# The scales of a sequence, turned one resume later behind the last of their powers, in a convolution, attention and state-space kernel

## The chip, the cores and the metric

One core of one Trainium2 chip runs the whole kernel. The metric is the device time of one execution in microseconds (us), the median over several runs. The time before is the median of three.

## The reference

The input `x` is 4 images of 128 channels and 64 x 64 pixels, in float32. Layer 0 normalizes it by groups and adds three convolutions (7x7, 5x5, 3x3), a non-local attention block and the input. Layer 1 takes the 4096 pixels of an image as a sequence of tokens of 128 features, and the change lies there:

```python
t = _to_tokens(x)                       # 4 sequences, 4096 tokens, 128 features
t = t + _L1_attn_ref(_ln_t(t), ...)     # h_f + h_b, a scan forwards and one backwards
t = t + _L1_ffn_ref(_ln_t(t), ...)      # projection, batch norm, a sigmoid recurrence

def _ln_t(v, eps=1e-5):
    m = jnp.mean(v, axis=-1, keepdims=True)
    s = jnp.var(v, axis=-1, keepdims=True)
    return (v - m) / jnp.sqrt(s + eps)
```

Both halves of layer 1 begin with a layer norm over the 128 features of a token, so each token needs one scale, 1/sqrt(variance + eps). (The mean is taken care of in the weights, which the kernel centres.) `_L1_attn_ref` is a state-space layer in each direction: a projection, a convolution of 4 taps, gates, and a scan with per-token decays `dt` and `dA`. The time steps `dt` come from the normalized tokens through a softplus, that is from exponentials and logarithms.

## The kernel before, in words

**Layout.** `t` lies in the on-chip memory with the 128 features on the partitions and all 4 x 4096 tokens along the free axis. The scan of layer 1 is `mamba`: 4 sequences b of 32 steps i of 128 tokens each, 128 steps n in all. Four steps make a group G, and j = i % 4 is the place in the group. A step does `states`, `turn`, `scan`, `prepare` and `take` (L1011 to L1066) for its own tokens, and, depending on j, a part of the projections of the next group (`project_bwd`, `project_bc`, `project_fwd`, `project_z`, L891 to L951) or of the finishing of the last one (`squares`, `means`, `gate`, `back`, L1068 to L1150). The step of j=1 is the one with `px` (L928, read by VectorE in L938), `pm` (L1087, read by VectorE in L1089) and `pb` (L901).

**Scales.** `row_scales` is a generator. It first runs `row_statistics`: for each of eight blocks of 512 tokens TensorE transposes four tiles of 128 x 128 into PSUM (`ls_in`, L83), VectorE takes mean and variance (L85 to L89), and GpSimd raises variance + eps to the power of -0.5 (`mr`, L74); after each block it yields. When all blocks are done it turns the 128 x 32 scales into 32 x 128 with one TensorE transpose (`rs_t`, L101), ScalarE copies them out of PSUM (L103), and SyncE sends them to device memory (L104), from where they are read back as rows that are broadcast over the partitions (`spread`, L109).

It is called in four places:

- L481, for the first sequence, whose tokens layer 0 leaves early, resumed in the loops of the attention block.
- L1161, in `open_sequence`, which prepares sequence b+1 while sequence b is being scanned. The generator of the opening is resumed at the end of each step from i=4, twice per step in i=4 to 7, so that the eight blocks are done in i=4 to 7, and `rs_t` follows in i=8. Behind it come the broadcasts `tl<-scale` (L109), three empty resumes (L1163), the products of scale and token (`scaled`, L727, two per resume, on GpSimd), and then `steps` (L798 to L888): `pd` in i=16 (projection to dt, L811), `pdt` in i=17 (its transposes, L821, read by VectorE in L825), the absolute value and the exponential in i=18 (L832 to L837), the logarithm and what follows it up to `dA` in i=19 (L839 to L847), `pcs` and `pt` in i=20 (running sums, L860 to L867), `pr` and the store of them in i=21 (L879 to L885).
- L1172, in `ended`, for the sequence before the present one, whose tokens are final by then: resumed once a step from i=20, so its eight blocks are in i=20 to 27 and its `rs_t` in i=28.
- L1331, in `recurrence`, run through at once.

The last sequence has its own blocks of statistics ahead of the recurrence (L1268 to L1271): steps 24, 25, 28 and 29 of the last sequence do one block each, behind the resume of `ended`.

**What sets the order.** TensorE and ScalarE run the scan in the order in which the code issues their instructions (`manual_schedule`, L787 and L788), so a yield decides in which step, and behind what, an instruction stands. VectorE, GpSimd and SyncE are put in order by a scheduler. All three queues run strictly in order, each instruction waiting for what it needs. Products of the openings, the gates and the state updates `S` (L1026) share GpSimd. The opening, the statistics, the projections and `pm` take their PSUM buffers from one pool, `ring`, of three:

```python
ring = ctx.enter_context(tc.tile_pool(name="m_ring", bufs=3, space=PSUM))
...
pt = ring.tile([P, MT, GT, QT], F32, tag="big", name="pdt")
```

Of the kernel before, what the change touches and what calls it, by code (L numbers as in the profile page):

```python
# [70 lines left out]
def rsqrt(nc, k, out, in_):  # L71

    p, n = in_.shape
    nc.gpsimd.tensor_tensor(out, in_, k.neghalf[:p].to_broadcast([p, n]), ALU.pow)  # L74


def row_statistics(nc, k, ps, tag, pool, src, mr, parts=None):

    for j in range(mr.shape[1] // GT) if parts is None else parts:
        pt = ps.tile([P, GT, P], F32, tag=tag, name="ls_in")  # L80
        st = pool.tile([P, GT, nc.vector.BN_STATS_DIM], F32, tag="ls_st", name="ls_st")
        for i in range(GT):
            nc.tensor.transpose(pt[:, i, :], src[:, ds(j * NC + i * P, P)], k.ident)  # L83
        for i in range(GT):
            nc.vector.bn_stats(st[:, i, :], pt[:, i, :])  # L85
        for i in range(GT):
            nc.vector.bn_aggr(mr[:, j * GT + i, :], st[:, i, :])
        v = mr[:, bass.ts(j, GT), 1]
        nc.vector.tensor_scalar(v, v, LN_EPS, None, ALU.add)  # L89
        rsqrt(nc, k, v, v)  # L90
        yield


def row_scales(nc, k, ps, tag, pool, src, mr, mem, parts=None):

    yield from row_statistics(nc, k, ps, tag, pool, src, mr, parts)
    n = mr.shape[1]
    pt = ps.tile([n, P], F32, tag=tag, name="rs_t")  # L100
    nc.tensor.transpose(pt, mr[:, :, 1], k.ident)  # L101
    row = pool.tile([n, P], F32, tag="rs_row", name="rs_row", bufs=1)
    nc.scalar.copy(row, pt)  # L103
    nc.sync.dma_start(mem, row)  # L104
# [48 lines left out]
def conv_attention(nc, tc, k, a, t, B, H, W, flags, load, mem, loads):  # L153
# [22 lines left out]
    with ExitStack() as ctx:  # L176
# [272 lines left out]
        for n in range(N):  # L449
# [17 lines left out]
            for i, _ in enumerate(convolve(n // 2, q % 2)):  # L467
                if i == 0:
                    if q % 2 == 0 and n:
                        for m in (n - 2, n - 1):  # L470
                            finish(m, atts.pop(m))
                        cv.pop(n // 2 - 1)
                    atts[n] = divide(n, acc, es)
                if more:
                    part = keys(b + 1, i)
                    next(part)
                if i == 2 and n + 1 < N:
                    th = queries(n + 1)
                if i == 3 and n == NQ + 1:
                    mr = wk.tile([P, NT, 2], F32, tag="mr", name="mr", bufs=1)  # L480
                    stats = row_scales(nc, k, ps_c, "c", wk, t[:, 0:T], mr, mem)  # L481
                if i == 3 and n > NQ:
                    next(stats, None)
                if more:
                    run(part)
# [204 lines left out]
def mamba(nc, tc, k, a, t, B, T, vec, first=None, after=None, mr=None):  # L690
# [16 lines left out]
    with ExitStack() as ctx:  # L707
# [447 lines left out]
        def open_sequence(b):  # L1155

            src = t[:, b * T : (b + 1) * T]
            if b not in tls:
                mr = pre.tile([P, NT, 2], F32, tag="mr", name="mr", bufs=1)
                mem = dram.tile([NT, P], F32, tag="scale", name="scale")  # L1160
                yield from row_scales(nc, k, ring, "big", wk, src, mr, mem)  # L1161
                scales(b, mem)
                for _ in range(3):  # L1163
                    yield
            if b not in ready:
                yield from scaled(b)
                yield
            yield from steps(b, ready[b])

        def ended(b):  # L1170
            mr = pre.tile([P, NT, 2], F32, tag="mr2", name="mr2", bufs=1)
            return row_scales(nc, k, ring, "big", wk, t[:, b * T : (b + 1) * T], mr, after[b])  # L1172
# [375 lines left out]
```

## Time and profile before

| | before |
|---|---|
| median of three runs | 3434.59 us (3430.04 to 3438.03) |
| profiled execution, span | 3440.8 us, mean granted TensorE clock 0.980 |
| instructions | 43618 |

The median is what counts; the profiled execution took a little longer than it. The profile lists for each engine how long it was busy, and which groups of instructions took that time. The trace behind it gives the start and length of each instruction and, where its engine stood idle ahead of it, the length of that wait in brackets and what ended it (an engine, a tile, a line of the kernel). Layer 0 takes the first part of the span and the scan roughly from 1.9 to 3.3 ms; the share of ScalarE, VectorE and GpSimd differs much between the two, so averages over the span say little on the scan. All that the change moves in the scan lies in a few steps of each sequence, of some 10 us each, and is read from the timelines of those steps:

| `rs_t` of | start, us | wait of TensorE ahead of it, us |
|---|---|---|
| first sequence, in layer 0 | 1079.69 | 0 |
| next sequence, first opening, i=8 | 2024.34 | 0 |
| next sequence, second opening, i=8 | 2364.80 | 0 |
| `ended` for the third sequence, i=28 | 3261.86 | 5.38 |
| recurrence | 3309.94 | 0.79 |

### The profile page before, as it was taken

To read this page: it belongs to the slowest core of one execution; us is meant where nothing else is said; L and a number is where in the kernel's file an instruction comes from. 1 tells how busy PE (TensorE), PEld (TensorE's weight loads), DVE (VectorE), ACT (ScalarE), POOL (GpSimd) and SP (SyncE) were. 2 spreads that over 40 slices of the span, in tenths; PEclk is the share of its full clock that TensorE was granted. 3 is DMA by queue.
4 is the path that set the end of the run, shared out by engine and by line. 5 is a ranking of instruction groups with operands and counts; after the bars stand their busy time and mean duration, and the time that the engine had idled before them with its cause. 6 is when DMAs were issued, how large, how long until landed. Compare 5 with 4: busy or idle time off the path is not lost. (4 is left out here: it accounts for less than half of the span.)

```text
span 3440.8 us, 43618 instructions
## 1 busy us (share of the span) xinstructions
PE 3261.0 (95%) x16823; PEld 1717.0 (50%) x16823; DVE 2138.7 (62%) x3204; ACT 1557.9 (45%) x2060; POOL 1593.3 (46%) x1414
## 2 busy tenths in 40 slices
PE   7999999999999999999998899999999999999976
PEld 2554545555555555455554344444444444544445
DVE  7555445555545555455544676777677777777767
ACT  3323233323333333333322566666656566666556
POOL 3434332534343424242533265557446654565653
PEclk9999999999999999999999899999999999999988
DMA  4000000000000000000001233333333423333332
GB/s 164 1 1 1 1 1 1 0 1 1 1 1 1 0 1 1 1 1 1 1 1 48 74 111 80 96 87 111 86 81 96 111 80 81 95 94 89 85 109 99
DMA packets 91685, 162.71 MB, mean 47 GB/s; under 512 B 23822, under 2 KB 27534, under 8 KB 90316
## 3 DMA queue, kind: packets, MB, share of 16 engines
q1 hardware_dynamic: 90252, 158.53, 16.2%
q8 instruction: 134, 2.20, 0.3%
q10 hardware_dynamic: 1216, 1.31, 0.1%
q14 instruction: 83, 0.68, 0.1%
HBM read 149.97 MB, written 9.82 MB: 46 GB/s over the span
## 5 line engine op out<-in xcount | busy, mean ns | idle before, releaser
L369 ACT ACTIVATE ex<-pf 128x1024 f32<-128x1024 f32 x512 | 497.0, 1021 | 571.6 <-PE pf L367 559.3
L384 DVE TENSOR_TENSOR es<-es,ex 128x1024 f32<-128x1024 f32 x448 | 590.6, 1318 | 207.5 <-ACT ex L369 179.4
L367 PE MATMUL pf<-theta,phi 64*128 64x512 f32 x2048 | 513.3, 619 | 10.8 <-ACT ex L369 10.4
L319 PE MATMUL pm<-yf,w 128*128 128x256 f32 x2048 | 503.1, 380 | 0.0
L378 PE MATMUL acc<-ex,gT 128*64 128x512 f32 x2048 | 491.4, 606 | 0.2 <-ACT ex L369 0.2
L331 POOL TENSOR_TENSOR eo<-s 128x256 f32<-128x256 f32 x128 | 90.1, 725 | 782.4 <-ACT s L328 782.4
L319 PEld LDWEIGHTS pm<-yf,w 128*128 128x128 f32 x2048 | 383.9, 189 | 113.5 <-issue 54.3
L367 PEld LDWEIGHTS pf<-theta,phi 64*128 64x128 f32 x2048 | 174.0, 186 | 326.7 <-ACT ex L369 208.6
L1007 POOL TENSOR_TENSOR ct<-ct,Cst 128x512 f32<-128x512 f32 x128 | 181.3, 1417 | 323.0 <-DMA ct<-csmem 261.9
L334 DVE TENSOR_TENSOR eo<-eo,pm 128x512 f32<-128x512 f32 x64 | 44.0, 688 | 425.8 <-PE pm L319 397.1
L378 PEld LDWEIGHTS acc<-ex,gT 128*64 128x64 f32 x2048 | 127.5, 136 | 337.5 <-issue 327.2
L969 DVE TENSOR_TENSOR lt<-cs,lt 128x1024 f32<-128x1024 f32 x128 | 180.5, 1411 | 182.3 <-DMA lt<-csmem 171.7
L328 ACT COPY s<-pm 128x512 f32<-128x512 f32 x64 | 37.5, 585 | 498.6 <-PE pm L319 498.6
L286 POOL TENSOR_TENSOR yf<-yr 128x340 f32<-128x340 f32 x256 | 241.4, 963 | 4.9
L914 PE MATMUL px<-tl,wx_fwd 128*128 128x512 f32 x512 | 238.6, 609 | 0.0
L901 PE MATMUL pb<-tl,wbc_bwd 128*64 128x512 f32 x512 | 235.1, 601 | 0.0
L901 PE MATMUL pb<-tl,wbc_fwd 128*64 128x512 f32 x512 | 234.5, 601 | 0.0
L286 POOL TENSOR_TENSOR yr<-xp 128x700 f32<-128x700 f32 x64 | 100.4, 1569 | 277.8 <-PE pm L319 232.0
L1072 POOL TENSOR_TENSOR yT<-yT,zT 128x512 f32<-128x512 f32 x127 | 183.8, 1456 | 74.1 <-DVE yT L1059 58.7
L1006 DVE TENSOR_TENSOR lt<-lt,gm 128x1024 f32<-128x1024 f32 x128 | 187.6, 1465 | 1.3
L390 DVE RECIPROCAL att<-den 128x512 f32<-128x512 f32 x32 | 107.4, 3357 | 108.0 <-PE den L388 108.0
L319 PE MATMUL pm<-yr,w 128*128 128x256 f32 x512 | 162.6, 398 | 0.0
(263 smaller groups left out, 5488.1 us busy)
## 6 DMA issues: line engine op xcount, KB each, us to landing
lt<-csmem SPq DMA_DIRECT2D x128, 512.0 KB, 5.5
ct<-csmem SPq DMA_DIRECT2D x256, 128.0 KB, 5.3
rs<-m SPq DMA_DIRECT2D x31, 512.0 KB, 3.7
t<-in_x SPq DMA_DIRECT2D x4, 2048.0 KB, 28.5
rows<-after SPq DMA_DIRECT2D x32, 256.0 KB, 4.8
out<-t SPq DMA_DIRECT2D x4, 2048.0 KB, 11.4
tl<-scale SPq DMA_DIRECT2D x24, 256.0 KB, 6.4
w<-in_w7t SPq DMA_DIRECT2D x1, 3136.0 KB
```

Source lines behind the costliest of these rows:

```text
L286: nc.gpsimd.tensor_tensor(out, at(x), at(y), op)
L319: nc.tensor.matmul(pm[:, e, :], wt, src, start=(i == 0), stop=(i == len(terms) - 1))
L367: nc.tensor.matmul(pf[:, e, :], phi[HALF[e], m, :], th[HALF[e]], start=True, stop=True)
L369: nc.scalar.activation(ex, pf, AF.Exp, scale=scale)
L378: nc.tensor.matmul(acc[HALF[e]], gT[:, 2 * m + e, :], ex[:, e, :], start=(m == 0), stop=(m == NT // 2 - 1))
L384: nc.vector.tensor_tensor(es, es, ex, ALU.add)
L901: nc.tensor.matmul(out, w[i]["bc"][:, tap, bass.ts(c, DS)], src, start=(tap == 0), stop=(tap == KC - 1),)
L914: nc.tensor.matmul(px, w[0]["x"][:, tap, bass.ts(c, P)], tl[:, rows(g, 0, tap)], start=(tap == 0), stop=(tap == KC - 1),)
L969: nc.vector.tensor_tensor(m["lt"], m["b"]["cs"][:, :, m["i"], :].unsqueeze(3).to_broadcast([P, ND, NHEAD, P]), m["lt"], ALU.subtract,)
L1006: nc.vector.tensor_tensor(lt, lt, gm.unsqueeze(2).to_broadcast([P, ND, NHEAD, P]), ALU.mult)
L1007: nc.gpsimd.tensor_tensor(m["ct"], m["ct"], Cs[:, cols].unsqueeze(1).to_broadcast([P, NHEAD, P]), ALU.mult)
L1072: eng.tensor_tensor(v, v, gr["z"][d][:, :, half(d, j // 2)], ALU.mult)
```

## The change

The generator gives way once more between the last block of statistics and the turn of the scales. The aim is that the power of the last block, which GpSimd may take late, is there when TensorE gets to the transpose, so that TensorE does not stand in front of it.

```diff
@@ row_scales
     yield from row_statistics(nc, k, ps, tag, pool, src, mr, parts)
+    yield
     n = mr.shape[1]
     pt = ps.tile([n, P], F32, tag=tag, name="rs_t")
     nc.tensor.transpose(pt, mr[:, :, 1], k.ident)
```

All that a caller does behind the scales moves with it. In `open_sequence` `rs_t` goes from i=8 to i=9, the products from i=11 to 14 to i=12 to 15, `pd` from i=16 to 17, `pdt` from 17 to 18, the exponential from 18 to 19, the logarithm from 19 to 20, `pcs` and `pt` from 20 to 21, and `pr` from 21 to 22. In `ended` `rs_t` goes from i=28 to i=29. In the attention loops of layer 0 it stands one resume later. In the recurrence nothing moves. The instructions are the same but for three loads of a function table on ScalarE (L833), which are no longer needed. On VectorE the chain from L840 to L847 lies in the step of i=21, behind the four L1059 of that step, and L869 goes ahead of the third L938. On SyncE the first `scale` goes behind `m<-ms`, `col<-m`, `lt` and `m<-col` of its step.

## The prediction

> **What bounds the kernel now.** I read the page's busy line, then the TensorE timeline around every `rs_t`, then each step of the scan that carries a piece of the next sequence's opening. The busy line (engine, busy us, share, instructions) and the clock row:
>
> ```profile
> PE 3261.0 (95%) x16823; PEld 1717.0 (50%) x16823; DVE 2138.7 (62%) x3204; ACT 1557.9 (45%) x2060; POOL 1593.3 (46%) x1414
> ...
> PEclk9999999999999999999999899999999999999988
> ```
>
> TensorE issues without pause nearly everywhere. A late result on VectorE or GpSimd counts only where TensorE stands. It stands little before `rs_t`. In the TensorE timeline (start, duration, engine, line, operation, in brackets the idle time ahead and what ended it), the turn for sequence 1 and the last turn of the scan are
>
> ```profile
> 2024.34 0.27 PE L101 MATMUL rs_t<-ident,mr 128*32 128x128 f32 x1
> ...
> 3261.86 0.40 PE L101 MATMUL rs_t<-ident,mr 128*32 128x128 f32 x1 [5.38 <-POOL mr L74]
> 3262.06 1.06 PE L83 MATMUL ls_in<-ident,t 128*128 128x128 f32 x4
> ```
>
> The seven other `rs_t` of the run wait under 1 us each; only this one stands 5.38 us. GpSimd's timeline there says why:
>
> ```profile
> 3256.38 3.47 POOL L1149 TENSOR_TENSOR t<-t,rs 128x512 f32<-128x512 f32 x2
> 3259.81 2.00 POOL L74 TENSOR_TENSOR mr<-mr,neghalf 128x4 f32<-128x4 f32 x1
> ```
>
> The power stands behind two updates of `t`. The larger stops lie in the openings, at the ring of three PSUM buffers (sequence 1, step i=17, TensorE, then the VectorE instructions that free a buffer):
>
> ```profile
> 2120.39 0.66 PE L821 MATMUL pdt<-ident,pds 128*128 128x128 f32 x4 [0.89 <-DVE ms L1089]
> 2123.76 1.11 PE L821 MATMUL pdt<-ident,pds 128*128 128x128 f32 x4 [2.71 <-DVE xT L938]
> ```
>
> ```profile
> 2119.66 0.67 DVE L1089 TENSOR_SCALAR ms<-pm 2x512 f32<-2x512 f32 x1
> ...
> 2122.97 0.74 DVE L938 SCALAR_TENSOR_TENSOR xT<-px,taps_bwd,xT 128x512 f32<-128x512 f32 x1
> ```
>
> A step with i%4=1 uses the ring for `px`, `pm` and `pb`, so whatever else asks there for a buffer waits until VectorE has read `pm` (L1089) and `px` (third L938). That is a property of the step, not of `pdt`.
>
> Without an opening, steps with i%4 = 0, 1, 2, 3 take 11.76, 10.15, 10.85 and 7.13 us (measured from the first `y` matmul to the next step's). With the opening of sequence 1, i=12, 16, 17, 18, 19, 20, 21 take 14.84, 13.61, 16.24, 11.89, 8.24, 13.73, 11.12.
>
> **What the Trainium skill says.** "TensorE: Matmul & The Clock Gate", What's actually happening: TensorE falls to half its clock after an idle window of about 3.4 us and needs about as long busy to get back. The windows agree: 3260.00 to 3266.60, behind the 5.38 us wait, has a granted clock of 0.50, and 2125.00 to 2130.00 has 0.51. Here even the 2.71 us stop is followed by half clock. So a stop costs more than itself: 6.8 us at half speed is 3.4 us of work lost. "ScalarE: Activation LUTs", What ACT_TABLE_LOAD costs: some 1283 ns; L833's three loads took 1283 ns each. "Trainium Kernel Development and Optimization", Best Practices, warns against judging TensorE by its busy share; that is why I count stops and step lengths, not the 95%.
>
> **The change, part by part.** No instruction is added but a yield of a generator; each `row_scales` gives its turn of the powers one resume later, and whatever its caller does afterwards moves by one step too.
>
> *Layer 0's turn.* One call, for the first sequence. TensorE's `rs_t` there (1079.69) costs 0.27 us wherever it stands, and its row is needed only in the scan, some 0.8 ms later: 0 us. The recurrence runs the generator through at once: 0 us.
>
> *Turn of the next sequence, i=8 to i=9.* It waited 0 at i=8, since its last power was issued at i=7. 0.27 us removed, 0.27 added: 0.
>
> *Table loads.* The Abs/Exp pair moves from the i=18 to the i=19 end of step, where the exp table is in place: three loads of 1.28 us are gone. ScalarE is 45% busy and TensorE's wait for it at i=20 is about 1 us. I count it within the steps below.
>
> *Broadcasts and products, i=11..14 to 12..15.* In the changed order SyncE issues `m<-ms`, `col<-m`, `lt` and `m<-col` ahead of `scale`; so the eight `tl<-scale` issues (4.01 us in a row) come behind them, and the eight products L727 (1.09 us each, 8.7 us) get to GpSimd at about 2048 instead of 2036. There they share the queue with `yT` products (1.3 to 1.75 us each), ahead of the state update S of i=12. Behind S on that queue waits VectorE's L1029, and for that TensorE's L991. That stop was 1.37, 1.35 and 0.62 us; I put S at 2057.9 and the stop at about 2.9 in sequence 1, partly repaid because the `rs` chain runs earlier. +0.8 each (0 to +2.5), three times: +2.4.
>
> *`pd`, `pdt`, i=16, 17 to 17, 18.* i=16 loses `pd`: 13.61-11.76 = -1.85. At i=17 `pd` (1.93 us) stands where `pdt` (0.66+1.11) stood, with the same two buffers: 0.89+2.71 of waiting stay, so does the half clock; +0.1. At i=18 `pdt` comes behind the four `pz`, whose buffers ScalarE frees at once: +1.5 with the half clock. i=19 loses its 1.11 of excess, of which the table load is part: -0.8. Sum -1.1 each (-2.5 to +0.5): -3.3.
>
> *`pcs`, `pt`, `pr`, i=20, 21 to 21, 22.* This is the largest term. At i=20 they found buffers free; at i=21 `pcs` takes the place of `pr`, and needs `dA` besides a buffer. In the changed VectorE order the Ln chain (L840 1.74, L841 0.62, L842 0.89, L844 0.41, L847 0.96, summed 4.6 us) stands behind `yT` of i=21 and has ms 0.67, gm 0.41, L1006 1.20, L935 0.2 to 0.9 and L969 1.23 between. `yT` ends about 3.7 us into the step, so `dA` is ready at 3.7+4.6+3.7 to 4.4, less overlaps of some 0.08 at each start, about 11.4 to 12.1. TensorE gets there at 8.85 (2170.36-0.75-2160.78). Stop of some 2.9. `pt` then waits for the third L938, which now stands behind L869, the reader of `pcs`: about 1 more. The work of `pcs` and `pt` is 1.25 us, at half clock 2.5, and the next two groups are slowed too: 6.8 over the 10.15 of the step. With 1.4 for i=22 (`pr` 0.4 and the rest of half clock) and 0.7 left at i=20: 8.9. Before, the three steps stood 1.97+0.97+0.43 = 3.4 above plain ones. +5.5 for sequence 1. In sequences 2 and 3 step 21 carries a statistics block of `ended` as well and already stopped 4.61 and 3.93 us (17.02 and 16.45 against about 11.5): 7.5 before against 8.6, +1.1 each. Sum +7.7 (-1 to +14).
>
> *`ended`, i=28 to 29.* The 5.38 us at 3261.86 goes away for `rs_t`. But the next in TensorE's order is `ls_in` of the last sequence's own block 2, which reads `t` written by the second L1149, done at 3259.85. TensorE was free at 3256.48. So 3.37 us of the 5.38 come back as a wait for `t`: -2.0 (-6, if the half clock goes too, to 0, if the 1.75 us wait for S at 3275.20 takes it up). `rs_t` at i=29 finds a power that is 10 us old. The turns of sequences 0 and 1 waited 0: 0.
>
> Sum: 2.4-3.3+7.7-2.0 = +4.8; 3434.6+4.8 = 3439.
>
> **Rivals.** *The full wait at i=21 (slower).* If `dA` is late by 5 instead of 2.9 us and GpSimd's products delay S at i=12 by all of 2.5 each: 14+7.5-3.3-2 = +16, 3451. For it: VectorE is 62% busy over the run and 7 tenths in this stage, L969 waits for a DMA in the same queue, and each stop of 2 to 3 us drew half clock. Against: VectorE idles 2.4 us in step 21 before, which the Ln chain can fill.
>
> *The waits come apart (faster).* `pd` needs only one freed buffer early, and `tl`, not VectorE; if at i=17 VectorE, which no longer has L825 between its L938, is done before TensorE asks, 2.7 us of stop and 1.7 of half clock go, three times 4.4 = 13.2. With -6 at the end: 2.4-3.3-13.2+7.7-6 = -12, 3422. For it: the change takes the one long wait in front of an `rs_t`, and the three table loads. Against: the four L825 that vanish there took 0.13 to 0.2 us each, and L938 was late because of a DMA (L969 waited 3.28 us ahead of it).
>
> **How the numbers follow.** Small net loss or nothing, 0.43, 3439; full wait, 0.37; waits come apart, 0.20. A measurable difference begins 6.9 us away (3427.7, 3441.5). The likeliest case is near the upper bound, and its part above it, some 0.06, is offset by the part of the full wait that stays below; so slower 0.37, same 0.43, faster 0.20. The range reaches to both rivals' values, 3424 to 3452, and leaves out their far halves.
>
> **What would show it.** The `rs_t` of i=29 without a wait and an `ls_in` at i=28 with 3.4 us behind L1149: the end term is right. A `pd` at i=17 with about 3.6 us behind L1089 and L938: the ring, not `pdt`, makes that stop. A `pcs` at i=21 waiting for L847: the main loss; if it waits under 1 us, the forecast is too high by 6 or more. L991 at i=12 standing under 1.5 us makes the first term nothing. TensorE instructions of the conv stage that stop behind `rs_t` would make it wrong altogether.

## The result, and the profile after

The changed kernel took 3440.39 us (median of four runs, 3434.63 to 3445.00), the kernel before beside it 3436.31 us (four runs, 3430.04 to 3440.71). The ratio is 1.0012, with a 95% interval of 0.9990 to 1.0035: 4.1 us more, which a measurement of this kernel can't tell from no change. The forecast was 3439, a sum of +4.8 us. The total fits. The terms behind it don't, and the rest of this text is about that.

The page of the changed kernel, busy line and clock row:

```profile
PE 3265.9 (95%) x16823; PEld 1717.6 (50%) x16823; DVE 2132.4 (62%) x3204; ACT 1554.5 (45%) x2057; POOL 1598.0 (46%) x1414
...
PEclk9999999999999999999999899999999999999988
```

ScalarE has three instructions less, the table loads. Nothing else on this page tells of a change; one has to go to the steps. The tile view of `rs_t` (L102 now) lists what TensorE and its weight loader waited for, with the sum in us and the number of waits:

```profile
  PE rs_t L102: 13.6, 3
  DVE ms L1090: 4.3, 5
  POOL mr L74: 1.9, 2
```

In the kernel before, the waits for `mr` were 12.8 us by the same count, which holds each wait once for TensorE and once for its weight loads. So the aim of the change is met: hardly any `rs_t` waits for its power. The end of the scan, in TensorE's timeline (idle time ahead and its cause in brackets), answers to the line with 5.38 us:

```profile
3262.96 1.11 PE L83 MATMUL ls_in<-ident,t 128*128 128x128 f32 x4 [4.43 <-POOL t L1150]
...
3270.68 0.30 PE L102 MATMUL rs_t<-ident,mr 128*32 128x128 f32 x1
```

```profile
3259.42 3.49 POOL L1150 TENSOR_TENSOR t<-t,rs 128x512 f32<-128x512 f32 x2
3262.87 2.00 POOL L74 TENSOR_TENSOR mr<-mr,neghalf 128x4 f32<-128x4 f32 x1
```

The second fence is GpSimd's. The `ls_in` behind it now waits for the second update of `t`, 4.43 us, and the two clock-halved groups behind it remain (1.12 us each for L1018 and L982 where 0.65 is usual). The wait has changed hands.

The openings changed more. In the first one, `rs_t` ran at 2034.83 in place of 2024.34. TensorE and then GpSimd in the steps i=9 to 12:

```profile
2034.83 0.30 PE L102 MATMUL rs_t<-ident,mr 128*32 128x128 f32 x1
...
2059.38 0.48 PE L992 MATMUL small<-ident,Bst 128*128 128x128 f32 x1 [3.45 <-DVE S L1030]
```

```profile
2048.40 2.25 POOL L728 TENSOR_TENSOR tl<-tl,t 128x512 f32<-128x512 f32 x2 [1.62 <-DMA tl<-scale]
2050.61 1.28 POOL L1073 TENSOR_TENSOR yT<-yT,zT 128x512 f32<-128x512 f32 x1
2051.84 2.08 POOL L728 TENSOR_TENSOR tl<-tl,t 128x512 f32<-128x512 f32 x1
2053.87 1.28 POOL L1073 TENSOR_TENSOR yT<-yT,zT 128x512 f32<-128x512 f32 x1
2055.10 3.19 POOL L728 TENSOR_TENSOR tl<-tl,t 128x512 f32<-128x512 f32 x3
2058.25 0.62 POOL L1027 TENSOR_TENSOR S<-S,tot 128x256 f32<-128x256 f32 x1
```

```profile
2058.90 0.42 DVE L1030 TENSOR_TENSOR S<-S,small 128x256 f32<-128x256 f32 x1 [3.57 <-POOL S L1027]
```

Six products of scale and token and two `yT` stand without a gap ahead of S; TensorE stands from 2055.9 until VectorE, which waited for GpSimd's part (last line), has added to S. In the kernel before TensorE also waited for S in this step, 1.37 us, but for another reason. GpSimd, VectorE and TensorE there:

```profile
2053.80 0.61 POOL L1026 TENSOR_TENSOR S<-S,tot 128x256 f32<-128x256 f32 x1
...
2055.37 1.29 DVE L1146 TENSOR_TENSOR rs<-rs,po 128x512 f32<-128x512 f32 x2 [1.49 <-DMA rs<-m]
2056.57 0.41 DVE L1029 TENSOR_TENSOR S<-S,small 128x256 f32<-128x256 f32 x1
...
2057.04 0.33 PE L991 MATMUL small<-ident,Bst 128*128 128x128 f32 x1 [1.37 <-DVE S L1029]
```

GpSimd's part of S was ready at 2054.41. VectorE's part stood behind two L1146, which waited for `rs`. The chain to `rs` ran late there: its transfer `col<-m` was issued at 2042.77, behind those of the scales, and the power of `col` (L74) ran on GpSimd at 2048.73, behind all eight products. In the changed kernel they come ahead of both, at 2036.00 and 2039.31, and L1147 (the same line) does not wait. So the change takes away one stop at i=12 and puts a longer one in its place. The other two openings read the same.

Behind the stop of the changed kernel the clock is halved: by windows (length, busy us and instructions of each engine, clock, DMA share, GB/s),

```profile
2054.24:2059.40 5.16, 1.71 (x33) 1.30 (x33) 1.59 (x4) 0.00 (x0) 5.16 (x6) 0.94 0.72 163
2059.40:2066.20 6.80, 6.80 (x17) 2.31 (x19) 5.75 (x10) 2.33 (x3) 6.80 (x5) 0.55 0.13 39
```

And the steps i=17 and 21 of that opening, on TensorE, with the VectorE instructions around `pcs`:

```profile
2121.20 1.07 PE L812 MATMUL pd<-tl,wdt 128*32 128x512 f32 x8
2124.82 1.07 PE L812 MATMUL pd<-tl,wdt 128*32 128x512 f32 x8 [2.54 <-DVE xT L939]
...
2168.97 0.49 PE L861 MATMUL pcs<-xe,tri 128*128 128x128 f32 x2 [2.86 <-DVE xe L848]
2169.30 0.39 PE L862 MATMUL pcs<-xe,after 128*128 128x128 f32 x2
...
2170.06 0.44 PE L868 MATMUL pt<-xe,ones 128*64 128x128 f32 x4
```

```profile
2168.64 0.48 DVE L848 TENSOR_TENSOR xe<-dt,A 128x128 f32<-128x128 f32 x2
2169.04 1.52 DVE L939 SCALAR_TENSOR_TENSOR xT<-px,taps_bwd,xT 128x512 f32<-128x512 f32 x2
2170.49 0.41 DVE L870 COPY cs<-pcs 128x256 f32<-128x256 f32 x1
```

`pd` waits where `pdt` waited, and `pcs` waits for `dA` by 2.86 us. But `pt` does not wait, and in this opening neither stop is followed by half clock: `pcs` is at its usual 0.39 us after the first pair. In the second and third openings `pcs` waits for something else, the PSUM buffer that L1090 (L1089 before) frees, 2.48 us in both, and the block of `ended` behind it for L939, 0.84 and 1.92 us; half clock follows there.

A profile is one execution, and steps that several kernels have alike differ between their profiles by up to 2.7 us, as stops and half clock fall. The 14 profiles of this study share most of their steps, so each place can be read from several of them. A step goes from its first `y` matmul to that of the next; the three openings are summed:

| steps | as before, us | as changed, us | difference |
|---|---|---|---|
| i=12 (`rs_t` at i=8 against 9) | 38.9 (eight profiles, 37.5 to 40.5) | 53.5 (three, 52.4 to 54.9) | +14.6 |
| i=15 to 24 (`pd` at 16 against 17) | 348.6 (five, 346.0 to 350.9) | 339.9 (four, 337.4 to 343.4) | -8.7 |
| i=28 to 30, last sequence only | 26.5 (seven) | 24.7 (six) | -1.9 |

The sum is +4.0, beside the 4.1 us measured; each term is known to some 2 us, so the agreement is closer than it need be. Of the +14.6, TensorE's stops for S make 2.7 us per opening (3.7 against 1.0, means of the same profiles), which leaves 2.2 for the half clock behind them. By step, the -8.7 is made of i=16 -5.5, 17 -0.9, 18 +1.2, 19 -4.1, 20 -6.5, 21 +6.9, and some +0.2 for 22 to 24.

### The profile page after: what moved, and what is told of

Same layout as the page of the kernel before. It is cut to its first block, busy times and chain, and to the rows that moved or that the text cites. A ratio compares the mean times of both kernels' runs of the same rounds, so it can differ in the third digit from the quotient of the medians.

```text
span 3443.3 us, 43593 instructions
## 1 busy us (share of the span) xinstructions
PE 3265.9 (95%) x16823; PEld 1717.6 (50%) x16823; DVE 2132.4 (62%) x3204; ACT 1554.5 (45%) x2057; POOL 1598.0 (46%) x1414
## 5 line engine op out<-in xcount | busy, mean ns | idle before, releaser
L329 ACT COPY s<-pm 128x512 f32<-128x512 f32 x64 | 37.5, 586 | 498.6 <-PE pm L320 498.6
L1007 DVE TENSOR_TENSOR lt<-lt,gm 128x1024 f32<-128x1024 f32 x128 | 185.8, 1451 | 1.3
```

Source lines behind the costliest of these rows:

```text
L1007: nc.vector.tensor_tensor(lt, lt, gm.unsqueeze(2).to_broadcast([P, ND, NHEAD, P]), ALU.mult)
```

## The experiments

### The parts of the change, alone

Is it the turn or the later half of the opening that costs? Both move by one step in the change, and can be moved apart. First the turn without the rest:

```diff
 def row_scales(..., late=False):
     yield from row_statistics(nc, k, ps, tag, pool, src, mr, parts)
+    if late:
+        yield
...
-                yield from row_scales(nc, k, ring, "big", wk, src, mr, mem)
+                yield from row_scales(nc, k, ring, "big", wk, src, mr, mem, late=True)
                 scales(b, mem)
-                for _ in range(3):
+                for _ in range(2):
                     yield
```

> The kernel before, with the extra yield in the openings only, and one of the three empty resumes behind it taken out: rs_t at i=9, but pd, pdt, pcs and pr stay at i=16, 17, 20 and 21. Theory A (the later turn puts the scale transfer behind the m<-col transfer on SyncE's queue, the products come late to GpSimd, and S of i=12 stands behind them): TensorE's stop at i=12 is 3.4 to 4.1 us as in the changed kernel and the three steps i=12 are 14 us longer together, while steps 16 to 22 are as before; +14 us, ratio about 1.004. Theory B (as forecast: the turn costs about 0.8 us per opening, and what moves the time is the later half of the opening): +2 us, 1.0007.

Measured: 1.0036 (1.0023 to 1.0050), 3448.01 us, 12 us more than before (differences in this part follow from the ratio). The steps i=12 sum to 53.4 us, with stops of 4.96, 3.45 and 2.69 us for S; steps 15 to 24 sum to 348.5, as before. The sizes are those of theory A, and the forecast's price of the turn fails. A's reason, the queue of SyncE, is looked at below.

Then the rest without the turn:

```diff
                 yield from scaled(b)
-                yield
+                for _ in range(2):
+                    yield
             yield from steps(b, ready[b])
```

> The kernel before, with rs_t left at i=8 and one more empty resume between the products and pd: pd, pdt, exp, ln, pcs, pr at i=17 to 22. Theory A (the later place of pd to pr is what gains, some 4.6 us per opening): i=12 as before, steps 16 to 22 shorter by 13.8 us in all; 3422 us, ratio 0.996. Theory B (as forecast, the move costs 1.5 us per opening): 3440, ratio 1.0013.

Measured: 0.9975 (0.9966 to 0.9984), 3423.53 us: 8.6 us less. i=12 is at 39.0, steps 15 to 24 at 339.5. The direction is A's. Its size, 13.8, was read from the one pair of profiles, and the kernel before was unlucky there with half clock; over several profiles it is the 8.7 of the table, which is what the run's time shows.

And `ended` alone (`late=True` at its call only):

> The kernel before, with the extra yield in ended only. Theory A (the wait for the power changes hands: the next ls_in waits for the second L1149): the stop at i=28 of the last sequence stays at 3.4 to 4.4 us, the gain is 1 to 2 us; ratio 0.9995. Theory B (the wait and the half clock behind it go): -5.4-3.4 = -8.8 us, ratio 0.9974.

Measured: 0.9986 (0.9980 to 0.9993), 3429.95 us, 4.8 us less, between the two. In its trace `ls_in` of i=28 waits 3.50 us for the second update of `t`, so the wait is handed on as A says; the steps 28 to 30 are 3.2 us shorter than in the one profile of before.

The three parts add to +12.4 - 8.6 - 4.8 = -1 us, each uncertain by 2 to 5 us; the whole change has -3 to +12. They agree.

### Why i=12 grows

Half of the products given to VectorE, in the changed kernel; the order of the products on the other engine's queue stays the same but for those that left:

```diff
-                eng = nc.vector if b == 0 and j % 3 < 2 else nc.gpsimd
+                eng = nc.vector if (b == 0 and j % 3 < 2) or (b and j % 2) else nc.gpsimd
```

> The changed kernel, with every second product of scale and token in sequences 1 to 3 done by VectorE in place of GpSimd; GpSimd's order is else the same. Theory A (the stop at i=12 is S standing behind six products on GpSimd): three products fewer ahead of S, 3.3 us, so TensorE's stop at i=12 falls from 3.5 to 4.1 us to under 1 us and the step from 18.3 us to 13 us; 12 to 15 us less than the changed kernel in all, ratio to before 0.997. Theory B (S is late for another reason): the stop stays over 2.5 us, ratio 1.001.

Measured: 1.0003 (0.9992 to 1.0013), 3437.11 us. The three steps i=12 fall to 35.3 us, the 11.76 of a plain step each: no stop for S at all. But steps i=11 grow from 21.6 to 34.4. TensorE, then VectorE:

```profile
2046.04 0.33 PE L992 MATMUL small<-ident,Bst 128*128 128x128 f32 x1 [3.23 <-DVE S L1030]
...
2055.39 0.33 PE L992 MATMUL small<-ident,Bst 128*128 128x128 f32 x1
```

```profile
2044.39 1.27 DVE L728 TENSOR_TENSOR tl<-tl,t 128x512 f32<-128x512 f32 x1 [5.02 <-DMA tl<-scale]
2045.58 0.41 DVE L1030 TENSOR_TENSOR S<-S,small 128x256 f32<-128x256 f32 x1
```

The product was placed ahead of VectorE's part of S and waited there 5.02 us for its row to land. So the cause at i=12 of the changed kernel is shown (take products away ahead of S, and the stop is gone), and the gain was lost to the same kind of stop one engine and one step earlier. The expectation of 0.997 missed that.

Does the queue of SyncE make the products late, or the turn itself? The `m<-col` transfer that `scale` stood behind was moved to GpSimd:

```diff
-            nc.sync.dma_start(m2, col)
+            (nc.gpsimd if gr["at"][1] == 1 else nc.sync).dma_start(m2, col)
```

> The changed kernel, with the one m<-col transfer of the second group of each sequence issued by GpSimd in place of SyncE, so that the scale transfer isn't queued behind it. Theory A (the queue on SyncE makes the products late): scale is issued 3 us or more earlier, the products follow, the stop at i=12 is under 1.5 us; 8 to 12 us less than the changed kernel, ratio 0.998 to 0.999. Theory B (the turn itself, 10 us later, makes them late, and the queue adds little): the stop at i=12 stays above 2.5 us; ratio 1.000 to 1.001.

Measured: 1.0007 (0.9998 to 1.0015), the stops at i=12 stay (3.28, 3.44 and 4.17 us). `scale` was issued 3.0 us behind `rs_t` in place of 6.6. But the `tl<-scale` transfers stood behind `rs<-m`, which waits for the transfer moved, and the first product began 13.4 us behind `rs_t`, against 13.6. So the experiment moved the wait to the next transfer of the same queue and does not settle the question. The lengths in the two traces of the first opening say more: from `rs_t` to the first product it was 11.8 us before and is 13.6 us after. Of the 12.3 us by which the first product came later, 10.5 are the turn and 1.8 the way from there, the queue included. So most of the lateness is the turn.

The turn the other way, one step earlier than before:

```diff
-            if i == 4:
+            if i == 3:
                 opening = ...
-            if i >= 4:
-                run(islice(opening, 2 if g == 1 else 1))
+            if i >= 3:
+                run(islice(opening, 2 if i < 7 else 1))
...
-                for _ in range(3):
+                for _ in range(4):
                     yield
```

> The kernel before with the opening begun at i=3, two resumes a step in i=3 to 6, and one more empty resume behind the turn: statistics and rs_t one step earlier (rs_t at i=7), pd to pr as before. The reverse of the change's move of the turn. Theory A (the time of the turn sets when the products come to GpSimd, and S of i=12 is late because of them): no stop at i=12, the step 11.8 us in each opening; 1 to 3 us less per opening there, ratio 0.998 to 0.999, less what the blocks cost at i=3. Theory B (the stop at i=12 is not the products'): it stays at 0.6 to 2 us; ratio 1.000.

Measured: 1.0037 (1.0024 to 1.0049), 3449.25 us. The stops at i=12 go, all three (35.3 us, 3.6 less than before), as A says. They go by another way than A's, though: the products are done before `col` comes, its power runs at 2037.35 in place of 2048.73, and `rs`, behind which S stood in the kernel before, is there in time. But now all eight products stand ahead of `zT`, on which `pm` of i=9 waits; steps i=9 grow from 30.4 to 53.1 us. GpSimd and TensorE in the first opening:

```profile
2016.89 8.42 POOL L727 TENSOR_TENSOR tl<-tl,t 128x512 f32<-128x512 f32 x8
2025.27 1.26 POOL L1081 TENSOR_TENSOR zT<-zT 128x512 f32<-128x512 f32 x1
```

```profile
2026.58 1.80 PE L1087 MATMUL pm<-zT,mean 128*2 128x512 f32 x2 [3.14 <-POOL zT L1081]
2030.01 1.86 PE L1087 MATMUL pm<-zT,mean 128*2 128x512 f32 x2 [1.63 <-POOL zT L1081]
```

With `rs_t` at i=8 the products cost least: only the chain to `rs`, and S behind it, is late then, for a stop of about 1 us. A step either way they meet something that TensorE waits for longer.

### Where the later half belongs

The forecast said that a step with i%4=1 has no free PSUM buffer and no free VectorE for an opening. Two more resumes ahead of `pd` (`range(3)` in the diff above) take the opening's TensorE work off both such steps:

> Two more empty resumes between products and pd: pd at i=18, pdt 19, exp 20, ln 21, pcs and pt 22, pr 23. Theory A (a step with i%4=1 has no free PSUM buffer for the opening until VectorE has read pm and px, and its VectorE queue is full; whatever opens there stops TensorE): steps 17 and 21 lose the opening's stops of 2.5 to 4.4 us and the half clock behind them; against one more resume another 4 us in the first opening and 6 in each of the other two; 3406 us, ratio 0.991. Theory B (the stops belong to pd and pcs themselves, which wait for ScalarE and VectorE wherever they stand): as with one more resume, 3422, 0.996, or worse.

Measured: 0.9952 (0.9938 to 0.9966), 3418.70 us, 16.5 us less than before. Steps 17 are plain (10.0 to 10.3 us), and 21 is 12.0 to 12.2. But 22 took much of it back, in the first opening so:

```profile
2170.61 0.77 PE L860 MATMUL pcs<-xe,tri 128*128 128x128 f32 x2 [3.94 <-DVE xe L847]
```

So each theory is right in part. The stop at 17 belonged to the step: `pd` does not stop at 18, and `pdt` at 19 stops 0.55 us. But `pcs` waits for `dA` in its new place as well (in the third opening too, 1.10 and 0.50 us), as the Ln chain still falls to VectorE in step 21, and in the second and third openings TensorE waits 1.37 us for S in step 22. Then one more empty resume between the chain and `pcs`:

```diff
             dA = flat(dA)
             yield
+            if b:
+                yield
```

> As with two more empty resumes before pd (pd at i=18, exp at 20, ln at 21), and one more between dA and pcs: pcs and pt at i=23, pr at 24. Theory A (pcs stops TensorE because VectorE has not a whole step for the Ln chain): no stop before pcs, step 22 falls from 18.0, 15.5 and 15.9 to about 11, 12.5 and 12.5 us; 3408 us, ratio 0.992. Theory B (the chain delays other VectorE results wherever it stands): steps 21 to 23 sum to the same; 3418, 0.995.

Measured: 0.9952 (0.9936 to 0.9969), the same. No stop before `pcs`, and the three steps 22 are 11.8 us shorter; but steps 23 and 24, which now carry `pcs` and `pr`, also stop for VectorE's `lt` (2.04 us in the first opening) and S (0.46 to 1.62 us in the others), and over steps 15 to 24 only 2 us are left. Theory B is the better one. That the chain of 4.6 us on VectorE delays something in a full step, whoever waits, fits it but was not tested further.

The place that follows from both has the chain in step 20, as before, and no TensorE work of the opening in 17 and 21:

```diff
                 yield from scaled(b)
-                yield
             yield from steps(b, ready[b])
...                                      (behind pdt)
             yield
+            if b:
+                yield
             nc.scalar.activation(e, x, AF.Abs)
...                                      (ahead of pr)
             yield
+            if b:
+                yield
             pr = p_g if b == 0 else ring.tile(...)
```

> The kernel before with the turn where it was, and the later half of the opening placed so that steps with i%4=1 have nothing of it to run: pd at i=15, pdt at 16, nothing at 17, exp at 18, ln at 19 (so that VectorE has the chain in step 20), pcs and pt at 20, nothing at 21, pr at 22. Theory A (in a step with i%4=1 both the PSUM buffers and VectorE are taken): step 17 falls by 5 to 6 us, 21 by 1 us in the first opening and by 4 to 5 us in the others, 20 stays, 15 and 16 sum to the same; 3412 us, ratio 0.993. Theory B (the stops of the opening are its own and move with it): 3425, 0.9975, as with one more resume before pd.

Measured: 0.9929 (0.9915 to 0.9942), 3412.81 us, 24 us less than before and faster than both kernels. Steps 15 to 24 sum to 328.3 against 348.6, and the total is A's. Its parts are less so: over the three openings 17 falls by 13 us and 21 by 7, less than put, 15 and 16 grow by 3, and 18 and 19 fall by 4, which was not put at all. None of its opening's TensorE groups waits over 0.3 us:

```profile
2103.97 1.03 PE L821 MATMUL pdt<-ident,pds 128*128 128x128 f32 x8
...
2147.00 0.38 PE L862 MATMUL pcs<-xe,tri 128*128 128x128 f32 x2
```

What stays in 21 is `ls_in` of `ended`, which waits some 2.2 us for the reader of `pm` (L1093 here, L1089 before) in the second and third openings.

### The end of the scan

If `ls_in` took over the wait at i=28, moving that block should take it away:

```diff
-            if mr is not None and b == B - 1 and i in (24, 25, 28, 29):
+            if mr is not None and b == B - 1 and i in (24, 25, 29, 30):
```

> The extra yield in ended only, and the last sequence's own blocks of statistics at steps 24, 25, 29 and 30 in place of 24, 25, 28 and 29. Theory A (at i=28 ls_in took over the wait from rs_t): no stop before ls_in at i=28, 3.5 us less than with ended alone and up to 3.4 us of half clock; ratio to before 0.997. Theory B (GpSimd sets the pace at the end of the scan): the wait comes back at i=29 or 30; ratio 0.9986 as with ended alone.

This is with the late turn in `ended`. Measured: 0.9991 (0.9983 to 0.9999), against 0.9986 without the move. There is no `ls_in` stop in step 28 (6.88 us against 9.02), but the first `y` of step 29 stops 2.44 us for `lt`, which VectorE had late, and the step is longer by 1.8. The ratio is theory B's, and a wait does come back at i=29, though not the one for `t`. What sets the pace at the end of the scan is not shown.

The yield in `ended` together with the better place, and with the earlier turn too:

> The same, with the extra yield of the change in ended alone. Theory A (the two add): another 4.8 us less, ratio 0.9915. Theory B (the end of the scan takes it up): as without, 0.993.

> The later half placed off the steps with i%4=1, the extra yield in ended alone, and the opening begun one step earlier. Theory A (three separate savings that add): ratio 0.990. Theory B (the earlier blocks cost as much as the earlier products save): as without, 0.9915.

Measured: 0.9938 (0.9925 to 0.9952) and 0.9968 (0.9955 to 0.9980). The yield in `ended` adds nothing that can be seen to the 0.9929, and the early turn costs as it did alone (i=9 at 51.0 us). So what `ended` is worth stays open within some us: 2.4 to 6.9 us by the run with it alone, nothing by the pair with the better place, 1.9 us by the steps of 13 profiles.

## Why the prediction was right, and where it was not

The total and the likeliest case, a small loss or nothing, were right: +4.8 by its sum, +4.1 measured, which can't be told from no change. Behind it one term was 12 us too low and two were 6 and 7 us too high. That they cancelled was luck.

- **Layer 0's turn, the turn itself, the recurrence: 0.** Right. TensorE's `rs_t` in the openings costs 0.30 us wherever it stands; the scan begins 0.5 us later than in the kernel before. Over the 14 profiles its beginning lies anywhere from 1924.3 to 1932.8 us, so nothing can be read from that, and no run moved layer 0's turn alone.
- **Broadcasts and products, +2.4.** Wrong, +14.6. What the products would do was forecast closely: S at 2057.9 (2058.25 measured), the first product at 2048 (2048.40), a stop of 2.9 us (3.45). The step that failed is the price put on it, "+0.8 each", in two ways. The stops of the kernel before ("1.37, 1.35 and 0.62 us") were read as S behind GpSimd's queue; they were VectorE waiting for `rs`. The changed kernel loses those when it gains the new ones, so taking the difference and then something "repaid because the `rs` chain runs earlier" counts one gain twice: the stops grew by 2.7 us per opening. And no half clock was put there, 2.2 us more. The prediction states, with the Trainium skill's "TensorE: Matmul & The Clock Gate", What's actually happening, that a stop costs more than itself, and used it at i=21, but not here. The page's idle window of about 3.4 us is not needed in full here: in these traces 1.4 us of idle within one window of 3.41 us brought half clock at times, and more than 2.05 us always (see the end).
- **`pd` and `pdt`, -3.3.** The direction was right, the size is -9.3 (i=16 to 19). i=16 gave the -1.85 forecast. i=17 kept its stop behind `px` (2.5 to 2.7 us), -0.3 each. i=18 cost 0.4 each where 1.5 was put, since `pdt` found buffers and less half clock, and i=19 gave 1.4 each where 0.8 was put. The term mis-sized most is i=18.
- **`pcs`, `pt`, `pr`, +7.7.** Wrong, +0.6 (i=20 -6.5, 21 +6.9, 22 to 24 +0.2). In the first opening `pcs` stopped 2.86 us where 2.9 was worked out. What failed are the things added to it: "`pt` then waits for the third L938, about 1 more" (it did not wait), "0.7 left at i=20" (a plain 11.76), and half clock for all behind ("at half clock 2.5", and 1.4 for i=22). The clock granted between 2168.90 and 2175.70 was 1.00. At i=12 the prediction left the half clock out where it came; here it put it in for the first opening, where it came in two profiles of the four with `pcs` at 21. In the second and third openings `pcs` took the wait for the buffer that `pr` had before, i=21 grew by 1.1 and 1.8 us, and i=20 gave 2.3 each, so the three steps there were no dearer than before, where +1.1 was put.
- **`ended`, -2.0.** Right within what can be read: -1.9 by the steps, -4.8 by the run with it alone, with the wait passed to `ls_in` as said, 4.43 us where 3.37 was put.
- **The rivals.** Of the slower one, given 0.37, the full wait at i=21 did not come; its other half, 2.5 us for S in each opening, did, and reached 4.9. Of the faster one, given 0.20, the waits at i=17 did not come apart. What neither contained was a large loss at i=12 with a gain behind it that pays for most of it.

That the later place of `pd` to `pr` gains is shown by the run with it alone. That the loss at i=12 is S behind the products is shown by the run that gives half of them to VectorE. The skill's table loads, "ScalarE: Activation LUTs", What ACT_TABLE_LOAD costs, are three loads of 1.28 us that fell away in just these steps, but they can be 0.2 us at most of i=19's gain of 1.4. In the kernel before VectorE waited only 0.21 us for the exponential behind such a load, and then worked without a gap until the second pair of L1059 had read `y`; 0.1 us later TensorE wrote to `y` again. The change takes L835 to L837, 2.4 us of VectorE's work in the first opening, out of that step.

## What to carry to other kernels

A yield in a generator that feeds an in-order engine moves everything behind it in that generator; the wait that it was meant for may be the smallest thing it moves. Look behind the name of a wait: TensorE waited for S at i=12 in both kernels, once for VectorE's `rs` and once for GpSimd's products. Price each moved piece by the step that it lands in (who has the buffers, which queue is full, who stands behind it), and try the pieces apart: here one half of the edit lost 12 us and the other gained 9, and the total hid both. Where the engine slows down behind a stop, count the slowdown at every stop of the sum, with the chance that it comes.

## What the runs showed that was not expected

- Whether half clock follows a stop depends on where the stop falls. In each trace the granted clock changes only on a fixed grid of 3.41 us: in the kernel before half clock begins at 2058.26 and at 2123.11, 19 such windows apart. In step i=21 of the first opening `pcs` stops 2.87 us in the kernel with the transfer moved to GpSimd, within one window, and the next window has half clock. In the changed kernel the 2.86 us are divided between two windows, and none has. The first two lines are of the former, the others of the latter:

```profile
2167.45:2170.86 3.41, 0.55 (x3) 0.18 (x2) 3.41 (x7) 2.39 (x3) 3.26 (x2) 1.00 0.00 0
2170.86:2174.28 3.42, 3.42 (x17) 2.44 (x18) 2.54 (x5) 1.17 (x3) 0.00 (x0) 0.50 0.02 1
...
2164.58:2167.99 3.41, 1.53 (x8) 0.30 (x4) 3.41 (x6) 3.36 (x4) 2.59 (x2) 1.00 0.02 2
2167.99:2171.41 3.42, 2.44 (x20) 1.80 (x20) 3.38 (x7) 0.65 (x4) 1.02 (x1) 1.00 0.02 1
2171.41:2174.82 3.41, 3.41 (x42) 2.31 (x41) 2.43 (x6) 3.01 (x5) 0.63 (x1) 1.00 0.19 56
```

- Over the scans of all 14 traces (1925 to 3300 us), every one of the 83 full-clock windows in which TensorE, by the busy time that the profile gives, idled more than 2.05 us was followed by half clock, none of the 5262 in which it idled less than 1.35 us, and 34 of the 78 between. Half clock lasted one, two or three windows. This is why one pair of profiles gave -13.8 for a term that is -8.7.
- Products on GpSimd take 1.09 us each when alone, but 2.08 us in the window where VectorE ran L1007, which took 2.12 us in place of 1.22. The forecast priced each at 1.09; whether one slowed the other was not tested.
- The best of these kernels differs from the one before by one empty resume taken out and two put in: 24 us, some six times what the change was worth either way.
